# A seven-sweep graph kernel on one core: other order of the last two product phases, feature loads one phase ahead on another queue, separate count buffers, and a longer manual order at the start

## The chip, the cores and the metric

The kernel runs on one core of a Trainium2 chip. The metric is the device time of one execution in microseconds (us). The kernel before takes 3252.63 us (median of 3 runs, 3252.13 to 3258.63). The chips differ a little: in the rounds of the experiments the same kernel before took between 3253 and 3260 us (medians), so kernels of different rounds are compared by their ratio to the kernel before, not by their times.

## The reference

A graph network of four layers over one 2708 x 2708 adjacency `adj` and 2708 x 512 features `x`, all in float32. The heavy work is seven products of an adjacency-sized matrix with a feature-sized one. Cut to that:

```python
def _L0_gnn_ref(cur, incidence_m):
    head = (incidence_m > 0).astype(incidence_m.dtype)
    head = head / jnp.maximum(jnp.sqrt(jnp.sum(head * head, axis=-1, keepdims=True)), EPS)
    inc = incidence_m + head
    return (inc @ cur) / jnp.sum(inc, axis=-1, keepdims=True)          # sweep 0
# layer 1: adj @ x, and attn @ h with
#   e = where(adj != 0, exp(-leaky_relu(s_left[:, None] + s_right[None, :], 0.01)), 0)
# layer 2: p = adj_norm @ p, three times, each hop with its own weight
# layer 3: relu((dinv * (adj + I) * dinv @ x + x) @ W + b),  deg = max((adj != 0).sum(-1), 1)
x = _layernorm(x + _L0_gnn_ref(x, adj), axis=-1)                       # and so after each layer
```

In sweep 0 the row of `head` needs the number of positive entries of each row before the product can start, so every adjacency block is loaded once more to be counted. And the attention of layer 1 needs `s_left` as a column and `s_right` as a row; the kernel writes values made from the first as columns in sweep 0 and reads them back as rows later.

## The kernel before

Each of the seven products is a *sweep*. The 2708 nodes are split in halves, so the adjacency has four quarters 11, 12, 21, 22 and the features have four quarters B11, B12, B21, B22. A sweep goes over four ranges of adjacency columns; for each range seven products (P1 to P7) of the Strassen-Winograd kind replace eight. A product takes one *phase*, a range 7 phases, a sweep 28. The very first range is "plain": eight ordinary products. Positions in the listing are in phases from the start of a sweep. They set the order of the list; a scheduler may move an instruction ahead of its place.

```python
RANGES0 = [(768, 256), (0, 384), (384, 384), (1024, 330)]
PLAIN = dict(P1=0, P7=1, P5=2, P6=3, P4=4, P2=5, P3=6)
STAT = dict(P1="B11", P7="T3", P5="T1", P6="T2", P2="B21", P4="T4", P3="B22")
MOV = dict(P1="11", P7="s3", P5="21", P6="11", P2="12", P4="22", P3="11")
RING = 46
...
    def trans(nm):
        return pool.tile([P, 384], F32, name=nm, tag="ring", bufs=RING)
...
    # features of the next sweep: four quarters per tile, then the four sums T1 to T4
    def next_x(base, src, direct, sums=0.95, halves=0.50):
        for k in range(KT):
            late = (k * P) >= RANGES[-1][0]
            q = nc.gpsimd
            f = k / KT
            if not late:
                at(base - 5.8 + f, lambda k=k: x_load(src, k, "B11", q))
                at(base - 0.89 + f, lambda k=k: x_load(src, k, "B21", q))
                at(base - 0.88 + f, lambda k=k: x_load(src, k, "B22", q))
                at(base - 0.87 + f, lambda k=k: x_load(src, k, "B12", q))
                at(base - 0.6 + f, lambda k=k: x_sums(k))
...
    # counts of sweep 0: load, mask (ScalarE or VectorE), count by a product with ones
    def count_load(R0, n, h, i):
        w = wt(i % KT)
        t = trans("cl")
        j0 = (i // KT) * NH + (i % KT) * P
        nc.sync.dma_start(out=t[:w, :n], in_=adjT[j0 : j0 + w, h * NH + R0 : h * NH + R0 + n])
        cnt[R0, h, i] = t
```

When a tile of sweep 0 is done, two columns of 128 values are stored by GpSimd as rows of a matrix `SR` in memory:

```python
                for m in range(2):
                    nc.gpsimd.dma_start(out=SROW[R0, h][m : m + 1, lo : lo + w].rearrange("a i -> i a"),
                                        in_=rcol[:w, t, m : m + 1])
```

Adjacency tiles are loaded by SyncE into a ring of 46 buffers. At the end of the program, manual dependencies keep the instructions of the first range (`[:strict]`) in the order of the list on each engine.

## Time and profile before

| | before |
|---|---|
| time, median of 3 | 3252.63 us |
| profiled span | 3258.3 us |
| TensorE busy | 3152.8 us, 97% |
| VectorE, ScalarE, GpSimd busy | 1590.9, 564.8, 328.0 us |
| start to the first product | 47.6 us |
| four ranges of sweep 0 | 109.5, 126.1, 129.8, 114.0 us |
| first range of sweep 1 | 130.4 us (123.4 in the shortest run below) |
| last product of the last sweep to the end | 21.5 us |

The length of a range is read on TensorE's timeline, from its first product to the first product of the next range. With TensorE at 97%, only its waits and its slow spells can be won back; the prediction goes through them. Two views that the prediction does *not* use should have been read as well. The first is the list of DMA issues of the kernel before (columns: out<-in, engine, operation, number, KB each, median us from issue to landing):

```profile
SR<-rcol POOLq DMA_DIRECT2D x40, 0.5 KB, 9.1
```

A store of half a kilobyte takes 9.1 us, where a store of 256 KB (`X<-o`) takes a median of 3.5 us. There are 44 of these column stores (4 more of 0.3 KB). The second is the DMA view of the kernel before from 176 to 200 us, in 40 slices of 0.6 us (busy tenths of the DMA engines, then GB/s moved):

```profile
DMA  3957771099039675528999363895265364891167
GB/s 72 411 239 77 255 287 37 13 72 13 0 74 46 18 31 41 41 41 272 378 364 74 44 33 90 143 138 72 74 141 146 87 248 100 256 371 64 51 97 259
```

From the seventh to the eighteenth slice (179.6 to 186.8 us) some slices are 90% busy, and yet no more than 74 GB/s pass, where the 2nd, 3rd, 5th and 6th slices before them and the 19th to 21st after them show 239 to 411. Four column stores are issued between 177.8 and 181.7 us. In the trace's records of single packets, the data packets of SyncE's queue take a mean of 928 ns and up to 5346 ns from 180 to 182 us, against 82 ns in the 2 us before.

### The profile page before, as it was taken

What the parts mean: (1) busy time and instruction counts of PE and PEld (TensorE: products, weight loads), DVE (VectorE), ACT (ScalarE), POOL (GpSimd) and SP (SyncE); (2) the same over time, 40 slices, a digit from 0 to 9 for tenths busy, and PEclk for the clock granted to TensorE, in tenths of its full rate; (3) what the DMA queues carried; (4) which work ended last, traced back from release to release, by engine and by line L of the source; (5) the groups of instructions that cost most, each with busy time, mean ns of one, the idle gap of its engine ahead of it and who ended that gap; (6) DMA issues with size and microseconds to landing.
All of it is one profiled execution on the core that took longest, in us unless ns stands there. A gap on an engine that the chain in (4) does not pass through costs nothing. (4 is left out here: it accounts for less than half of the span.)

```text
span 3258.3 us, 35588 instructions
## 1 busy us (share of the span) xinstructions
PE 3152.8 (97%) x12090; PEld 2049.5 (63%) x12090; DVE 1590.9 (49%) x3914; ACT 564.8 (17%) x1096; POOL 328.0 (10%) x571
## 2 busy tenths in 40 slices
PE   4899998999999999999999999999999999899998
PEld 3656565556765555765556865568656587555675
DVE  5677596243356775865232333223254343543444
ACT  2543400000044544631000000000000000000000
POOL 0002013000000011113000020000111011300000
PEclk9999998999999999999999999999999999999999
DMA  5767566322343332544333453324434344533340
GB/s 168 190 176 140 152 136 108 87 64 53 94 88 113 114 114 90 152 138 148 102 87 87 122 153 101 104 65 124 137 115 139 98 135 131 171 116 95 106 128 30
DMA packets 268613, 380.42 MB, mean 117 GB/s; under 512 B 34824, under 2 KB 231008, under 8 KB 268432
## 3 DMA queue, kind: packets, MB, share of 16 engines
q1 hardware_dynamic: 232612, 293.00, 34.3%
q0 software_dynamic: 27104, 74.33, 7.2%
q10 hardware_dynamic: 8716, 10.84, 1.0%
q8 instruction: 95, 1.56, 0.2%
q14 instruction: 86, 0.70, 0.1%
HBM read 322.53 MB, written 55.49 MB: 116 GB/s over the span
## 5 line engine op out<-in xcount | busy, mean ns | idle before, releaser
L256 DVE TENSOR_TENSOR a<-a,a 128x384 f32<-128x384 f32 (+4 forms) x963 | 474.8, 509 | 333.3 <-PE accu L289 162.2
L289 PE MATMUL accu<-a,B 128*128 128x384 f32 (+5 forms) x1188 | 370.4, 457 | 0.0
L289 PE MATMUL acca<-a,B 128*128 128x384 f32 (+5 forms) x1188 | 362.2, 452 | 0.0
L289 PE MATMUL accc<-s,T 128*128 128x384 f32 (+5 forms) x1188 | 359.7, 455 | 0.0
L289 PE MATMUL accd<-a,B 128*128 128x384 f32 (+5 forms) x1188 | 356.2, 454 | 0.0
L289 PE MATMUL accd<-a,T 128*128 128x384 f32 (+5 forms) x1188 | 355.1, 457 | 0.0
L289 PE MATMUL accc<-a,T 128*128 128x384 f32 (+5 forms) x1188 | 352.5, 453 | 0.0
L289 PE MATMUL accu<-a,T 128*128 128x384 f32 (+5 forms) x1188 | 350.1, 452 | 0.0
L289 PEld LDWEIGHTS accd<-a,T 128*128 128x128 f32 (+1 forms) x1188 | 226.6, 192 | 113.6 <-issue 4.8
L289 PEld LDWEIGHTS accu<-a,T 128*128 128x128 f32 (+1 forms) x1188 | 223.4, 190 | 109.0
L289 PEld LDWEIGHTS accd<-a,B 128*128 128x128 f32 (+1 forms) x1188 | 222.4, 191 | 107.1 <-issue 4.0
L289 PEld LDWEIGHTS acca<-a,B 128*128 128x128 f32 (+1 forms) x1188 | 220.4, 190 | 109.7 <-issue 14.4
L289 PEld LDWEIGHTS accc<-a,T 128*128 128x128 f32 (+1 forms) x1188 | 222.3, 190 | 106.2
L289 PEld LDWEIGHTS accu<-a,B 128*128 128x128 f32 (+1 forms) x1188 | 219.8, 191 | 105.4 <-issue 14.4
L289 PEld LDWEIGHTS accc<-s,T 128*128 128x128 f32 (+1 forms) x1188 | 220.3, 190 | 103.4 <-issue 3.9
L256 DVE TENSOR_TENSOR s<-a,a 128x384 f32<-128x384 f32 (+4 forms) x321 | 162.0, 509 | 187.2 <-PE acca L289 121.2
L330 DVE TENSOR_TENSOR W<-W,accd 128x384 f32<-128x384 f32 (+2 forms) x54 | 27.3, 510 | 318.7 <-PE accd L289 317.2
L371 POOL TENSOR_TENSOR rstd<-rstd,neg_half 128x1 f32<-128x1 f32 (+1 forms) x88 | 52.0, 591 | 1031.9 <-DVE rstd L370 1026.2
L716 DVE TENSOR_TENSOR e<-e,f 128x384 f32<-128x384 f32 (+5 forms) x176 | 88.3, 506 | 81.4 <-ACT f L715 79.4
L330 DVE TENSOR_TENSOR C<-U,accc 128x384 f32<-128x384 f32 (+2 forms) x54 | 27.2, 509 | 204.1 <-PE accc L289 203.1
L323 ACT COPY U<-accu 128x384 f32<-128x384 f32 (+2 forms) x54 | 23.8, 443 | 572.7 <-PE accu L289 571.4
L714 ACT ACTIVATE e<-row,neg_s 128x384 f32<-128x384 f32 (+5 forms) x176 | 101.0, 574 | 101.6 <-DVE a L717 39.3
(199 smaller groups left out, 3104.5 us busy)
## 6 DMA issues: line engine op xcount, KB each, us to landing
a<-in_adjT SPq DMA_DIRECT2D x560, 192.0 KB
a<-in_adjT SPq DMA_DIRECT2D x280, 165.0 KB
a<-in_adjT SPq DMA_DIRECT2D x273, 128.0 KB
cl<-in_adjT SPq DMA_DIRECT2D x80, 192.0 KB
ld<-X SPq DMA_DIRECT2D x60, 256.0 KB
Y<-y POOLq DMA_DIRECT2D x54, 256.0 KB, 2.6
B<-Y POOLq DMA_DIRECT2D x84, 128.0 KB, 3.1
X<-o POOLq DMA_DIRECT2D x36, 256.0 KB, 3.5
```

Source lines behind the costliest of these rows:

```text
L256: nc.vector.tensor_tensor(A[r, dst, k][:w, :n], A[r, a, k][:w, :n], A[r, b, k][:w, :n], op)
L289: nc.tensor.matmul(B[home, c][:, :n], X[STAT[p], k][:w, c * P : (c + 1) * P], A[r, MOV[p], k][:w, :n], start=bool(start and k == k0), stop ...
L323: nc.scalar.copy(T[nm, c][:, :n], B[home, c][:, :n])
L330: nc.vector.tensor_tensor(d[:, :n], T[t, c][:, :n], o[:, :n], ALU.add)
L371: nc.gpsimd.tensor_tensor(rstd[:w, 1:2], rstd[:w, 0:1], neg_half[:w], ALU.pow)
L714: nc.scalar.activation(e[:w, :n], row[R0, h][0][:w, :n], AF.Exp, bias=neg_s[:w, t : t + 1])
L716: nc.vector.tensor_tensor(e[:w, :n], e[:w, :n], f[:w, :n], ALU.min)
```

## The change

Its intent: take the waits out of the start of the program, of the counts in sweep 0 and of the boundaries between sweeps. The diff cut to its core (cuts are marked):

```diff
-PLAIN = dict(P1=0, P7=1, P5=2, P6=3, P4=4, P2=5, P3=6)
+PLAIN = dict(P1=0, P7=1, P5=2, P6=3, P4=4, P3=5, P2=6)
-RING = 46
+RING = 43
...                               # x_sums: T4, the one that needs B21, goes to x_last
+    def x_last(k):
+        w = wt(k)
+        nc.vector.tensor_tensor(new_x("T4", k)[:w], X["B21", k][:w], X["T2", k][:w], ALU.subtract)
...
-    def next_x(base, src, direct, sums=0.95, halves=0.50):
+    def next_x(base, src, sums=0.95, halves=-0.25):
+        q = nc.sync
         for k in range(KT):
...
-            q = nc.gpsimd
...
                 at(base - 5.8 + f, lambda k=k: x_load(src, k, "B11", q))
-                at(base - 0.89 + f, lambda k=k: x_load(src, k, "B21", q))
-                at(base - 0.88 + f, lambda k=k: x_load(src, k, "B22", q))
-                at(base - 0.87 + f, lambda k=k: x_load(src, k, "B12", q))
-                at(base - 0.6 + f, lambda k=k: x_sums(k))
+                at(base - 1.85 + f, lambda k=k: x_load(src, k, "B22", q))
+                at(base - 1.84 + f, lambda k=k: x_load(src, k, "B12", q))
+                at(base - 1.55 + f, lambda k=k: x_sums(k))
+                at(base - 0.85 + f, lambda k=k: x_load(src, k, "B21", q))
+                at(base + 0.1 + f, lambda k=k: x_last(k))
             else:                 # tiles of the last range
-                at(base + halves + 0.05 * (k - 8), lambda k=k: x_load(src, k, "B21", q))
-                at(base + halves + 0.01 + 0.05 * (k - 8), lambda k=k: x_load(src, k, "B22", q))
+                at(base + halves + 0.05 * (k - 8), lambda k=k: x_load(src, k, "B22", q))
+                at(base + max(halves, 0.1) + 0.05 * (k - 8), lambda k=k: x_load(src, k, "B21", q))
...
-        t = trans("cl")
+        t = pool.tile([P, 384], F32, name="cl", tag="cl", bufs=3)
...
-        at(pb + (5.6 if r else 3.3), lambda: run_sums(R0, n, 0, inverse, r > 0))
+        at(pb + (5.2 if r else 3.3), lambda: run_sums(R0, n, 0, inverse, r > 0))
...                               # last sweep
-        order = (2, 3, 0, 1) if h else (0, 1, 2, 3)
+        order = (2, 3, 0, 1)
...
-    for i in list(nc.cur_bb.bb.instructions)[:strict]:
+    for n, i in enumerate(list(nc.cur_bb.bb.instructions)[:3 * strict]):
         if i.engine in last:
             tc.add_manual_dep(i, last[i.engine].name, ...)
-        last[i.engine] = i
+        if n < strict:
+            last[i.engine] = i
```

More of the change, by code (lines that the diff above doesn't have):

```diff
@@ L157, in x_sums @@
         b = b12.pop(k)
-        b11, b21, b22 = (X[s, k] for s in ("B11", "B21", "B22"))
-        for d, i, j in (("T1", b, b11), ("T2", b22, "T1"), ("T4", b21, "T2"), ("T3", b22, b)):
+        b11, b22 = X["B11", k], X["B22", k]
+        for d, i, j in (("T1", b, b11), ("T2", b22, "T1"), ("T3", b22, b)):
             j = X[j, k] if isinstance(j, str) else j
@@ L182, in x_load @@
         eng.dma_start(out=t[:w], in_=q)
-    def next_x(base, src, direct, sums=0.95, halves=0.50):
+    def next_x(base, src, sums=0.95, halves=-0.25):
+        q = nc.sync
         for k in range(KT):
-            late = (k * P) >= RANGES[-1][0]
-            q = nc.gpsimd
             f = k / KT
-            if not late:
+            if (k * P) < RANGES[-1][0]:
                 at(base - 5.8 + f, lambda k=k: x_load(src, k, "B11", q))
-                at(base - 0.89 + f, lambda k=k: x_load(src, k, "B21", q))
-                at(base - 0.88 + f, lambda k=k: x_load(src, k, "B22", q))
-                at(base - 0.87 + f, lambda k=k: x_load(src, k, "B12", q))
-                at(base - 0.6 + f, lambda k=k: x_sums(k))
-            else:
-                at(base + halves + 0.05 * (k - 8), lambda k=k: x_load(src, k, "B21", q))
-                at(base + halves + 0.01 + 0.05 * (k - 8), lambda k=k: x_load(src, k, "B22", q))
-                if not direct:
-                    at(base + 0.3 + 0.1 * (k - 8), lambda k=k: x_load(src, k, "B11", q))
-                    at(base + 0.31 + 0.1 * (k - 8), lambda k=k: x_load(src, k, "B12", q))
+                at(base - 1.85 + f, lambda k=k: x_load(src, k, "B22", q))
[3 more added lines that the diff above has]
+                at(base + 0.1 + f, lambda k=k: x_last(k))
+            else:
+                at(base + halves + 0.05 * (k - 8), lambda k=k: x_load(src, k, "B22", q))
+                at(base + max(halves, 0.1) + 0.05 * (k - 8), lambda k=k: x_load(src, k, "B21", q))
                 at(base + sums + 0.03 * (k - 8), lambda k=k: x_sums(k))
+                at(base + sums + 0.4 + 0.03 * (k - 8), lambda k=k: x_last(k))
     def next_ext(base, src):
@@ L216, in rest @@
                 x_sums(k)
+                x_last(k)
             at(base + 1.05 + 0.2 * (k - KT), rest)
@@ L614, in gnn_kernel @@
         at(6.0 + 0.9 * f, lambda k=k: x_sums(k))
+        at(7.5 + f, lambda k=k: x_last(k))
     at(2.6, start0)
     sweep(S[0], KT, RANGES0, prep=prep0, extra=extra0, done=done0, first=True, sums=True)
-    next_x(S[1], X1, True)
+    next_x(S[1], X1)
     W = {}
@@ L731, in extra2 @@
         at(pb - 1.0, lambda: rows(1))
-        at(pb + 5.6, lambda: run_sums(R0, n, 0, share))
+        at(pb + 5.2, lambda: run_sums(R0, n, 0, share))
         at(pb + 2.6, lambda: run_sums(R0, n, 1, share))
@@ L823, in gnn_kernel @@
     for s, hop, src, done in ((3, 2, Y0, hop_done(Y1)), (4, 1, Y1, hop_done(Y2)), (5, 0, Y2, done5)):
-        next_x(S[s], src, True, *((1.3, 0.95) if s == 3 else (0.95, 0.5)))
+        next_x(S[s], src, *((1.3, 0.3) if s == 3 else (0.95, -0.25)))
         next_ext(S[s], w_hop[hop])
         sweep(S[s], KT + 2, RANGES, done=done, ext_src=X2T, late=1.4 if s == 3 else 0.85)
-    next_x(S[6], X3, True)
+    next_x(S[6], X3)
     def start6():
@@ L853, in pre @@
             nc.vector.tensor_tensor(y[:, :n], y[:, :n], t[:, :n], ALU.add)
-        order = (2, 3, 0, 1) if h else (0, 1, 2, 3)
-        early = {(1, 2): -0.95, (1, 3): -0.9, (0, 0): -1.0, (0, 1): -0.95}
+        order = (2, 3, 0, 1)
+        early = {(1, 2): -0.95, (1, 3): -0.9, (0, 2): -1.05, (0, 3): -1.0}
         for j, c in enumerate(order):
```

## The prediction

> **What bounds the kernel now.** I began with the page, to see which engine is full:
>
> ```profile
> PE 3152.8 (97%) x12090; PEld 2049.5 (63%) x12090; DVE 1590.9 (49%) x3914; ACT 564.8 (17%) x1096; POOL 328.0 (10%) x571
> PE   4899998999999999999999999999999999899998
> PEclk9999998999999999999999999999999999999999
> ```
>
> TensorE has work in 97% of the span. The change removes no product: all seven products of each range stay, only the last two swap places. So it can only win back idle or slow TensorE time. Idle is 3258.3 - 3152.8 = 105.5 us, and the slices put it in the first fifth and in one slice near the end. The waits view of TensorE names it:
>
> ```profile
> PE acca L299 <- DVE a L498: 20.6, 1, 20.6
> PE cnt L460 <- DVE mask L447: 20.3, 21, 3.8
> PE cnt L460 <- ACT mask L450: 20.0, 8, 5.6
> PE deg L654 <- DVE mask L642: 15.6, 3, 12.3
> PE ps_n L400 <- DVE U L330: 10.9, 4, 9.6
> ```
>
> (Columns: total us, times, longest.) These five are 87.4 of the 105.5 us; the last products' epilogue is most of the rest. Each was then followed back on the timeline of the engine it names.
>
> Start (20.6 us), VectorE's timeline:
>
> ```profile
> 25.16 0.22 DVE L472 TENSOR_SCALAR r<-cnt 128x1 f32<-128x1 f32 x2 [0.31 <-PE cnt L460]
> 30.24 3.66 DVE L162 TENSOR_TENSOR T<-T,B 128x256 f32<-128x256 f32 x10 [4.86 <-DMA T<-in_x]
> ...
> 41.94 4.58 DVE L162 TENSOR_TENSOR T<-B,T 128x256 f32<-128x256 f32 x13 [6.55 <-DMA B<-in_x]
> 46.43 0.42 DVE L497 SCALAR_TENSOR_TENSOR s<-a,row 128x256 f32<-128x256 f32 x1
> ```
>
> L162 is the feature sums, listed for phase 6 but hoisted into the first range. VectorE runs in order, so the adjacency preparation (L497, L498) that the first product needs stands behind sums that wait for the last feature quarters. ScalarE had copied its `row` by 26.96 + 0.37 = 27.3 us; the preparation starts at 46.4 and the first product at 47.58.
>
> Counts (20.0 us): ScalarE's timeline shows the masks waiting for the count tiles' load, here the longest:
>
> ```profile
> 328.32 0.48 ACT L449 ACTIVATE mask<-cl 128x330 bf16<-128x330 f32 x1 [7.17 <-DMA cl<-in_adjT]
> ```
>
> SyncE's timeline has 13 `cl` issues spread over 18.3 us from 313.6, against about 0.33 us for an issue that does not wait: the count tiles queue for slots of the ring that the adjacency tiles fill.
>
> First sweep boundary (15.6 us), TensorE, then VectorE:
>
> ```profile
> 522.61 0.24 PE L654 MATMUL deg<-ones_bf,mask 128*128 128x1 bf16 x3 [12.26 <-DVE mask L642]
> 510.30 0.43 DVE L162 TENSOR_TENSOR T<-B,T 128x256 f32<-128x256 f32 x1 [7.19 <-DMA B<-X]
> 517.30 0.43 DVE L162 TENSOR_TENSOR T<-B,T 128x256 f32<-128x256 f32 x1 [5.91 <-DMA B<-X]
> ```
>
> The next sweep's feature quarters load in the last phase, because the last product holds B22; GpSimd's issues alternate between waiting for TensorE, for VectorE and behind its small normalisation powers. VectorE, in order, stops at the sums and the masks behind them are late. The last boundary is the same (`ps_n` at 2818.42, 9.61 us, after `B<-X` waits in the chain). The four boundaries between lose about 1 us each or nothing.
>
> Two windows tell what else is near its limit:
>
> ```profile
> 160.00:200.00 40.00, 34.54 (x140) 20.59 (x138) 36.50 (x94) 13.89 (x28) 4.91 (x8) 0.94 0.79 170
> 520.00:560.00 40.00, 33.83 (x175) 21.14 (x176) 29.30 (x103) 2.76 (x6) 15.54 (x26) 0.84 0.42 64
> ```
>
> (Busy us of PE, PEld, DVE, ACT, POOL; granted clock; DMA share; GB/s.) At 160 to 200 us VectorE is busy 36.5 of 40. In both, the clock fell below 1.
>
> **What the Trainium skill says.** "TensorE: Matmul & The Clock Gate", section "What's actually happening": after an idle window of about 3.4 us the array runs at half clock until a busy one has passed. The trace agrees: after the 5.60 us wait at 329 us, twelve products of 128x384 take 6.89 us against 3.87 us elsewhere. So each long stall costs about 3 us more, and I count it with the stall. "DMA: Bandwidth & Descriptors", section "Issuing engines are not separate DMA queues": all issuers share the same 16 engines, and another issuer saves only issue time. So going from GpSimd to SyncE buys no bandwidth; it frees GpSimd (0.54 us busy per load in its timeline, a median 4.3 us from issue to landing for `B<-X`). "Advanced Engine Details and Errata", section "Sequencer Loop": a sequencer reads instructions one after the other. The trace agrees in the hoisted sums above; on SyncE it is also a risk.
>
> **The change part by part.**
>
> 1. *First range kept in order.* The manual dependencies now also hold the instructions listed up to three times as far behind the last one of the first range, which covers the sums at phase 6. Preparation can start at 27.3 instead of 46.4 us: 0.8 us for the first tile, first product at about 28.6. That is 47.6 - 28.6 = 19.0 us. Feeding it: B21 is issued from 19.8 to 26.1 us and needed one phase later (44 products of 0.216 us = 9.5 us); B22 had landed by about 42 to 46 us and is needed after three phases, about 59. So data should not stop it. But 33 subtractions (11 tiles of T1, T2, T4) at about 0.35 us, 11.6 us, return to VectorE between phases 6 and 8.5, just where it is 91% busy. I charge 4 us. Net 15.
>
> 2. *Count tiles in three buffers of their own, ring 46 to 43.* Waits at 188.9, 195.5, 318.7 and 329.4: 0.47 + 4.35 + 1.26 + 5.60 = 11.7 us, plus two half-clock spells of about 3.4 = 18.5 us. Count loads no longer hold ring slots, but stand in the same SyncE queue as adjacency loads that do, and three buffers allow no burst; near 195 us VectorE would set the pace anyway. I take 10. The waits in the first range (92.9 to 111.7 us, about 10 us idle) come from weight loads issued on ScalarE and from sums of weights; those stay.
>
> 3. *Order P3, P2, with B22 and B12 loaded and T1, T2, T3 formed one phase earlier; B21 and T4 later.* The last phase now holds only B21, which feeds T4, needed at phase 4. First boundary: 12.26 + 2.52 + 0.80 us of waits, and the window's clock of 0.84 gives 0.16 x 40 = 6.4 us, together 22. I take 18; masks and late tiles of the last range stay. Last boundary: 9.61 us and about 2.8 of slow clock; I take 11.
>
> 4. *Cost of the swap.* P3 needs 11-12, formed after the load of "12". Setting the third group of L256 against the start of the sixth phase, those combinations end before it in all 27 ranges (245.2 against 246.9 us in the tightest), so P3 one phase earlier should not wait. Moving the row sums from 5.6 to 5.2 is small for the same reason. The final epilogue mirrors the old one: 0.
>
> 5. *Smaller ring and the shared queue*: -1 to -5 us, most likely in the third sweep, where exponent tiles use the ring too. Freed GpSimd: +1 to 2. Together -2.
>
> Sum: 15 + 10 + 18 + 11 - 2 = 52; 3252.6 - 52 = 3200.6. The author has placed each event in fractions of a phase, which looks tuned on the chip, so I lean 2 us further: 3199.
>
> **Rivals.** *VectorE becomes the bound of the first sweep.* For: 36.5 of 40 us, and the sums come back there. Against: from 100 to 160 us the same windows show it busy 44.6 of 60. Then 1 and 2 give 10 instead of 25 us: about 3214. *SyncE's queue blocks at its head*: a feature load that waits for TensorE holds the next adjacency loads behind it. For: its timeline already has 32 `a` loads spread over 86.7 us from 498.9. Against: "11" slots are free a phase earlier in the new order, and no adjacency load is listed between the "12" loads and the last phase. Boundary gains would halve, and waits appear in the middle boundaries: about 3220. *All stalls vanish*: 19 + 18 + 22 + 12 = 71, with some of the first range's 10 us: about 3178, faster by over 2%. *Transfers hidden anyway*: the middle boundaries, a third of what was rewritten, gain nothing; already in the sum.
>
> **Range and chances.** The four gains are nearly independent, each uncertain by 4 to 7 us, together about 12, and I widen that for the rivals: 3178 to 3222. Two per cent is 65 us, 3187.6; that needs nearly every stall gone: 0.30. Within: 0.67. Slower: 0.03, as it would need new stalls of over 100 us.
>
> **What would show it.** Right: first acca product near 28 to 30 us; no mask wait for `cl` over 3 us after 160; PE waits of `deg` and `ps_n` at the two boundaries below 4 us; granted clock 0.95 or more in the window of the first boundary; `B<-X` gone from GpSimd. Wrong: waits of L289 for DVE L256 or L498 in the first sweep, waits for L162 sums at boundaries, new waits for `a` loads in the third sweep, or clock dips at other places.

## The result

The changed kernel takes 3272.39 us (median of 4 runs, 3267.95 to 3274.05) against 3253.01 us of the kernel before in the same rounds (4 runs, 3252.13 to 3258.63). The ratio is 1.0054 with a 95% interval of 1.0036 to 1.0071. Ratios in this document are the mean time of one kernel's runs over the mean of the other's in the same rounds, so they are not quite the ratio of the medians. The prediction of 3199 us is missed by 73 us, and the range by 50: instead of a gain of 54 us there is a loss of some 18.

The page of the changed kernel, whose profiled span is 3272.1 us (busy us of each engine; then, in 40 slices, the busy tenths of TensorE and the clock granted to it, in tenths of full speed):

```profile
PE 3172.4 (97%) x12090; PEld 2059.3 (63%) x12090; DVE 1593.8 (49%) x3914; ACT 571.2 (17%) x1096; POOL 225.4 (7%) x381
...
PE   6899998999999999999999999999999999899998
...
PEclk9899998999999999999999999999999999999999
```

The first slice went from 4 to 6 tenths, so the start is indeed shorter. GpSimd went from 328.0 to 225.4 us and from 571 to 381 instructions: the feature loads have left it. TensorE is busy 19.6 us *longer* with the same 12090 instructions, which is time at a slower clock: the clock record has 101.7 us at half speed, against 66.2 before, and half of the difference is 17.7 us. Its waits in the changed kernel (total us, times, longest; `cnt` is a count, `deg` a degree count, `ps_n` and `ps_t` are transposes of finished tiles, `accd` one of the large products, `ps_d` a product with a weight matrix):

```profile
PE cnt L463 <- ACT mask L453: 23.1, 9, 6.8
PE cnt L463 <- DVE mask L450: 19.5, 21, 4.0
PE ps_n L403 <- DVE P1c L333: 11.2, 2, 9.4
PE ps_t L409 <- DVE o L381: 10.4, 3, 9.1
PE accd L292 <- DVE a L259: 5.3, 3, 3.9
PE deg L658 <- DVE mask L646: 5.1, 2, 4.3
...
PE ps_d L417 <- DVE P1c L857: 2.7, 1, 2.7
```

Of the five lines of the prediction, the 20.6 us before the first product are gone. The other waits have moved rather than vanished: `deg` fell from 15.6 to 5.1 us, but `ps_t` (10.4), `accd` (5.3) and `ps_d` (2.7) are new, the waits of the counts for ScalarE's masks grew from 20.0 to 23.1 us, and the wait of `ps_n` at the last boundary is still there, at 9.4 instead of 9.6 us. The window of the first boundary (same columns as in the prediction) has not recovered either:

```profile
520.00:560.00 40.00, 32.91 (x176) 21.05 (x176) 25.16 (x89) 1.58 (x3) 9.09 (x15) 0.81 0.53 125
```

The granted clock there is 0.81, where it was 0.84.

The ledger of the two profiled runs, from the first products on TensorE's timeline, in us:

| stretch | before | after | difference |
|---|---|---|---|
| start to the first product | 47.6 | 27.6 | -20.0 |
| first range (plain) | 109.5 | 126.9 | +17.4 |
| second range | 126.1 | 125.8 | -0.3 |
| third range | 129.8 | 132.2 | +2.4 |
| last range of sweep 0 | 114.0 | 128.5 | +14.5 |
| first range of sweep 1 | 130.4 | 125.5 | -4.9 |
| from there to the last sweep | 2148.5 | 2149.7 | +1.2 |
| first range of the last sweep | 124.5 | 123.9 | -0.6 |
| rest of its ranges | 306.4 | 306.5 | +0.1 |
| epilogue | 21.5 | 25.5 | +4.0 |
| span | 3258.3 | 3272.1 | +13.8 |

So the start won what was predicted and the first range gave nearly all of it back; the last range of sweep 0 lost more than its boundary won; the epilogue lost 4 us. The traces name what stands behind each.

**First range.** ScalarE's waits in the kernel before, for the load of a count tile, over the whole run:

```profile
ACT mask L449 <- DMA cl<-in_adjT: 27.4, 7, 7.2
```

The same line after:

```profile
ACT mask L452 <- DMA cl<-in_adjT: 59.1, 28, 7.6
```

Seven waits have become 28, and 13 of these, 23.8 us, are in the first range. SyncE's own waits in the first range of the changed kernel (60 to 155 us) say why:

```profile
SPq L442 <- ACT mask L452: 46.5, 41, 10.6
```

The issue of a count load now waits for the mask that frees one of three buffers, 41 times.

**Last range of sweep 0.** SyncE's timeline after (start, us, engine, line, operation, out<-in, number):

```profile
433.56 2.28 SPq L249 DMA_DIRECT2D a<-in_adjT  x5
446.38 0.33 SPq L186 DMA_DIRECT2D B<-X  x1
446.81 14.43 SPq L249 DMA_DIRECT2D a<-in_adjT  x9
```

Between 435.84 (the end of the first line) and 446.38 SyncE issues nothing. It stands at one feature load; the program's order says that it is the B11 quarter of tile 5. Nine adjacency loads are behind it. GpSimd's timeline shows what the load waits for, the store of that same tile, and what the store waits among:

```profile
434.82 1.12 POOL L581 DMA_DIRECT2D SR<-rcol  x2 [0.56 <-DVE rcol L579]
435.93 0.54 POOL L393 DMA_DIRECT2D X<-o  x1
438.17 1.07 POOL L581 DMA_DIRECT2D SR<-rcol  x2 [1.70 <-DVE rcol L579]
```

The store `X<-o` sits between two pairs of column stores, and by the trace it lands at 446.36 us, 10.4 us after its issue. VectorE then runs out of adjacency tiles, at a load that SyncE issued right after it had stood (446.81) and that took 9.4 us more to land:

```profile
456.26 0.50 DVE L500 SCALAR_TENSOR_TENSOR s<-a,row 128x330 f32<-128x330 f32 x1 [8.58 <-DMA a<-in_adjT]
```

**First boundary.** At the end of that range the same happens again: SyncE stands 13.3 us, from 505.07 to 518.40, at a feature load that waits for an `X<-o` store. VectorE's timeline waits first for a fetch of `in_x` and then for the late B21:

```profile
517.86 0.75 DVE L557 SCALAR_TENSOR_TENSOR ld<-ps_n,rd,ld 74x512 f32<-74x512 f32 x1 [9.16 <-DMA ld<-in_x]
...
536.20 0.43 DVE L167 TENSOR_TENSOR T<-B,T 128x256 f32<-128x256 f32 x1 [7.82 <-DMA B<-X]
```

TensorE pays for the first of these with the 9.1 us of `ps_t` in its waits. The standing queue did not make this fetch late: SyncE had issued it at 503.63, before it stood, and it landed only at 517.84. The B21 load was as slow (issued 525.01, landed 536.18). These two waits are slow transfers, with column stores in flight, and not late issues.

**Last boundary.** SyncE, VectorE and TensorE in turn, each from its own timeline:

```profile
2805.42 7.24 SPq L186 DMA_DIRECT2D B<-X  x3
```

```profile
2814.02 0.43 DVE L167 TENSOR_TENSOR T<-B,T 128x256 f32<-128x256 f32 x1 [5.63 <-DMA B<-X]
```

```profile
2828.32 0.88 PE L403 MATMUL ps_n<-ident,P1c 128*128 128x128 f32 x2 [9.41 <-DVE P1c L333]
```

Three feature loads take 7.24 us to issue (0.33 us each when they do not wait), VectorE stands in order at T4, and the additions that feed the last tiles are behind it. Within the 7.24 us SyncE stands 5.9 us at a load that waits for an `X<-o` store. The first load that VectorE waits for was issued before that (2804.67) and took 9.3 us to land, so the block is not the whole of this wait.

**Epilogue.** TensorE after, at the output product of the last tiles:

```profile
3249.21 3.55 PE L417 MATMUL ps_d<-w,P1c 128*128 128x512 f32 x4 [2.66 <-DVE P1c L857]
```

Four products take 3.55 us where others of the form take 1.88, after a wait of 2.66.

### The profile page after: what moved, and what is told of

It reads as the page before. It is cut to its first block, busy times and chain, and to the rows that moved or that the text cites. A ratio compares the mean times of both kernels' runs of the same rounds, so it can differ in the third digit from the quotient of the medians.

```text
span 3272.1 us, 35367 instructions
## 1 busy us (share of the span) xinstructions
PE 3172.4 (97%) x12090; PEld 2059.3 (63%) x12090; DVE 1593.8 (49%) x3914; ACT 571.2 (17%) x1096; POOL 225.4 (7%) x381
## 4 chain that ended last, share of the span: by engine, by line
PE 88%; DMA 5%; DVE 3%; issue 1%; ACT 1%; POOL 0%; SPq 0%; ACTq 0%; POOLq 0%; DVEq 0%
PE accu L292 22%; PE accc L292 21%; PE accd L292 21%; PE acca L292 10%; PE ps_d L417 9%; DMA cl<-in_adjT 2%; PE ps_n L403 1%; DMA a<-in_adjT 1%; PE ps_t L409 1%; PE acca L302 1%; DMA ld<-in_x 1%; PE pz L683 1%; ACT mask L452 1%; DMA B<-in_x 0%; DMA B<-X 0%
## 5 line engine op out<-in xcount | busy, mean ns | idle before, releaser
L259 DVE TENSOR_TENSOR a<-a,a 128x384 f32<-128x384 f32 (+4 forms) x963 | 475.8, 510 | 370.0 <-DMA a<-in_adjT 194.9
L292 PEld LDWEIGHTS accu<-a,B 128*128 128x128 f32 (+1 forms) x1188 | 220.8, 192 | 107.4 <-issue 16.8
L259 DVE TENSOR_TENSOR s<-a,a 128x384 f32<-128x384 f32 (+4 forms) x321 | 161.9, 509 | 209.9 <-PE accd L292 102.6
L333 DVE TENSOR_TENSOR W<-W,accd 128x384 f32<-128x384 f32 (+2 forms) x54 | 27.1, 509 | 276.1 <-PE accd L292 262.3
L333 DVE TENSOR_TENSOR C<-U,accc 128x384 f32<-128x384 f32 (+2 forms) x54 | 27.1, 509 | 195.1 <-PE accc L292 193.7
```

Source lines behind the costliest of these rows:

```text
L259: nc.vector.tensor_tensor(A[r, dst, k][:w, :n], A[r, a, k][:w, :n], A[r, b, k][:w, :n], op)
L292: nc.tensor.matmul(B[home, c][:, :n], X[STAT[p], k][:w, c * P : (c + 1) * P], A[r, MOV[p], k][:w, :n], start=bool(start and k == k0), stop ...
L333: nc.vector.tensor_tensor(d[:, :n], T[t, c][:, :n], o[:, :n], ALU.add)
```

## The experiments

Four theories came out of this, against the prediction's own reasons as rivals.

- **A.** The column stores of sweep 0, which both kernels have, slow every other transfer for some 6 us each time. The waits that the prediction put down to ring slots (count tiles) and to the place of the feature loads (first boundary) were waits for these transfers. Rival: ring slots and places, as predicted.
- **B.** Three count buffers end the run-ahead of the count loads that the ring allowed. Rival: the subtractions that came back to VectorE made the first range long.
- **C.** SyncE issues in order; a feature load that waits for a store of `X` holds the adjacency loads and fetches behind it. Rivals: the new product order, or the earlier loads by themselves.
- **D.** The new order of the last sweep finishes feature chunks 0 and 1 last, but the output product still takes them first. Rival: the epilogue is longer for another reason.

All kernels gave correct results. The expectations sometimes count the ranges of a sweep from 0; the text and the tables count them from 1. In the names, "b" is the kernel before with something added, "a" the changed kernel with something altered. Times and ratios, with the median of the kernel before in the same rounds:

| run | median us | before | ratio to before, 95% |
|---|---|---|---|
| changed kernel | 3272.39 | 3253.01 | 1.0054 [1.0036, 1.0071] |
| b_twice | 3307.89 | 3254.25 | 1.0165 [1.0149, 1.0181] |
| b_rows | 3228.85 | 3260.24 | 0.9902 [0.9887, 0.9917] |
| a_rows | 3220.92 | 3260.24 | 0.9878 [0.9863, 0.9893] |
| b_strict | 3236.88 | 3254.25 | 0.9946 [0.9932, 0.9961] |
| a_clring | 3255.02 | 3260.24 | 0.9986 [0.9971, 1.0000] |
| a_pool | 3276.48 | 3260.24 | 1.0045 [1.0028, 1.0061] |
| a_clring_late | 3255.71 | 3259.63 | 0.9990 [0.9973, 1.0007] |
| a_clring_pool | 3250.12 | 3259.63 | 0.9966 [0.9951, 0.9981] |
| a_b11 | 3273.55 | 3259.74 | 1.0039 [1.0023, 1.0056] |
| a_clring_b11 | 3248.69 | 3259.74 | 0.9965 [0.9950, 0.9980] |
| a_rows_lateq | 3212.34 | 3254.25 | 0.9870 [0.9853, 0.9886] |
| a_dense (one look, state unknown) | 3280.87 | 3259.74 | none |
| a_clring_rows | 3207.86 | 3259.63 | 0.9837 [0.9822, 0.9852] |
| b_strict_rows | 3209.44 | 3259.63 | 0.9841 [0.9827, 0.9856] |
| best1 | 3197.78 | 3254.25 | 0.9827 [0.9812, 0.9842] |

The stretches in their profiled runs, in us, as in the ledger:

| run | first product | range 1 | range 2 | range 3 | last of sweep 0 | first of sweep 1 | epilogue |
|---|---|---|---|---|---|---|---|
| before | 47.6 | 109.5 | 126.1 | 129.8 | 114.0 | 130.4 | 21.5 |
| changed | 27.6 | 126.9 | 125.8 | 132.2 | 128.5 | 125.5 | 25.5 |
| b_twice | 45.0 | 125.8 | 130.9 | 140.2 | 133.4 | 132.4 | 21.5 |
| b_rows | 46.1 | 109.5 | 118.3 | 120.3 | 102.2 | 125.4 | 21.5 |
| a_rows | 27.9 | 115.3 | 118.5 | 120.2 | 105.1 | 123.4 | 25.7 |
| b_strict | 26.8 | 109.4 | 127.0 | 128.9 | 114.1 | 130.0 | 21.4 |
| a_clring | 27.0 | 109.3 | 128.9 | 135.6 | 124.5 | 125.1 | 24.0 |
| a_pool | 28.4 | 126.0 | 127.6 | 140.4 | 125.0 | 130.5 | 25.2 |
| a_clring_late | 27.5 | 110.7 | 127.2 | 132.7 | 126.0 | 125.2 | 24.0 |
| a_clring_pool | 26.4 | 111.2 | 129.8 | 126.6 | 119.9 | 131.3 | 25.4 |
| a_b11 | 28.1 | 128.4 | 128.7 | 136.3 | 124.3 | 126.4 | 25.7 |
| a_clring_b11 | 29.2 | 110.9 | 129.9 | 133.3 | 116.9 | 126.4 | 25.7 |
| a_rows_lateq | 26.9 | 117.5 | 118.6 | 120.2 | 105.4 | 123.4 | 25.6 |
| a_dense | 27.5 | 128.4 | 128.3 | 139.6 | 125.7 | 128.3 | 21.6 |
| a_clring_rows | 27.1 | 109.2 | 118.4 | 120.6 | 101.7 | 125.2 | 27.4 |
| b_strict_rows | 28.4 | 109.5 | 118.5 | 120.2 | 105.0 | 126.0 | 21.5 |
| best1 | 26.8 | 110.0 | 118.5 | 120.5 | 101.0 | 123.4 | 21.4 |

A control for reading it: the changed kernel and a_dense differ only in the last epilogue, yet their third ranges are 132.2 and 139.6 us, in different rounds (and a_dense is the look of unknown state). While the column stores are there, a single range of one profile says little below some 7 us. Without them, ranges 2 and 3 repeat within 0.4 us over six kernels.

### Theory A: the column stores

**b_twice**: the kernel before, each column store issued twice.

```diff
-                for m in range(2):
+                for m in (0, 1, 0, 1):
                     nc.gpsimd.dma_start(out=SROW[R0, h][m : m + 1, lo : lo + w].rearrange("a i -> i a"),
```

> The kernel before, with each column store of the first sweep issued twice (88 instead of 44, the same values; nothing else moves). Theory A: the waits grow with the number of column stores; taking them away saved some 31 us, so doubling them costs 15 to 40 us, ratio 1.005 to 1.012, all of it before 660 us. If their shape is harmless and it was only TensorE's and ScalarE's new place that helped in the row variant: within 4 us of before.

Measured: 3307.89 us, ratio 1.0165. That is 0.0165 x 3254 = 54 us for 44 more stores, 1.2 us per store, though they move 22 KB in all. It is in the expected direction and larger than the 15 to 40 us expected. All four ranges of sweep 0 grew, by 16.3, 4.8, 10.4 and 19.4 us; the first product and the epilogue did not.

**b_rows** and **a_rows**: TensorE transposes the two columns of a tile into two rows, ScalarE copies them, and one store writes two contiguous rows of 512 bytes.

```diff
-                for m in range(2):
-                    nc.gpsimd.dma_start(out=SROW[R0, h][m : m + 1, lo : lo + w].rearrange("a i -> i a"),
-                                        in_=rcol[:w, t, m : m + 1])
...                               # ps: the bank of tile "pg", made wider and handed on
+            def e(t=t, lo=lo, w=w, got=got):
+                ps = got["pg"]
+                nc.tensor.transpose(ps[:2, P : P + w], rcol[:w, t, :], ident[:w, :w])
+                s = small.tile([2, P], F32, name="srow", bufs=3)
+                nc.scalar.copy(s[:, :w], ps[:2, P : P + w])
+                nc.gpsimd.dma_start(out=SROW[R0, h][:, lo : lo + w], in_=s[:, :w])
...
+            at(p + 0.9, e)
```

For the kernel before:

> The kernel before, with the same row stores in place of the column stores. Theory A: the waits after 157 us for count tiles (11.7 us and two half-clock spells) and the first sweep boundary (22 us with its slow clock) go, the time falls from 3253 to about 3220. If the ring and the late feature loads were the cause, as my prediction had it, it stays within 5 us of 3253.

For the changed kernel:

> The changed kernel, with the 44 column stores of the first sweep (SR, 128 elements of 4 bytes each[...]) written instead as 22 row stores: TensorE turns the two columns, ScalarE copies them, one store of two rows. Theory A (the column stores hold up all other DMA traffic for some 6 us each, and that is what the count masks and the first sweep boundary wait for): the first range shrinks from 127.1 us to about 112, the last range of the first sweep from 128.5 to about 115, waits of the masks for count tiles fall from 59 us to under 25, and the time falls from 3272 to about 3230. Theory B (three count buffers) and theory C (feature loads that block SyncE's queue): the masks still wait, and the time stays within 8 us of 3272.

Measured: b_rows 0.9902, so 32 us faster than before; a_rows 0.9878, which against the changed kernel's 1.0054 is 1.76% or 57 us. The DMA issues of a_rows:

```profile
SR<-srow POOLq DMA_DIRECT2D x20, 1.0 KB, 2.9
```

The same values land in 2.9 us instead of 9. In b_rows, with ring, places and queues of the kernel before untouched, ranges 2 and 3 fall by 7.8 and 9.5 us, and the last range with its boundary by 11.8 + 5.0. So A holds in both directions, more stores and none, and the rival falls: no ring slot and no load was moved in b_rows. The packet records agree. Between the first product and the end of sweep 0, 399 packets of SyncE's queue take more than 1 us in the kernel before, 559 in b_twice and 14 in b_rows (of some 45000 in each). As these are SyncE's own loads, the time that GpSimd spends on issuing its stores does not explain them. The stores cost the changed kernel about 57 - 32 = 25 us more than the kernel before.

### Theory B: three count buffers

**b_strict**: the kernel before with the longer manual order alone.

```diff
-    for i in list(nc.cur_bb.bb.instructions)[:strict]:
+    for n, i in enumerate(list(nc.cur_bb.bb.instructions)[: 3 * strict]):
...
-        last[i.engine] = i
+        if n < strict:
+            last[i.engine] = i
```

> The kernel before, with the longer manual order alone (the change's part 1). The first product starts near 28 us instead of 47.6. Theory B (it was the three count buffers that gave this gain back): the first range keeps its 109.6 us and the whole is about 19 us faster than before, ratio 0.994. Rival (the order itself gives it back, as the sums return to VectorE): the first range or the second grows by 10 us or more and the ratio is 0.998 or above.

Measured: ratio 0.9946, 17.6 us. The first product comes at 26.8 us and range 1 stays at 109.4. So the subtractions that come back to VectorE cost nothing there, which removes the rival of B.

**a_clring**: the changed kernel with the count tiles in the ring again.

```diff
-RING = 43
+RING = 46
-        t = pool.tile([P, 384], F32, name="cl", tag="cl", bufs=3)
+        t = trans("cl")
```

> The changed kernel with the count tiles back in the ring of 46. Theory B (three buffers take away the run-ahead that covered slow stretches of DMA): the first range shrinks from 127.1 us to about 112 as the kernel before has it (109.6), and the time is about 3257. If the buffers are not it: 127 us and 3272.

Measured: ratio 0.9986; range 1 falls from 126.9 to 109.3 us, as in the kernel before. TensorE's waits in range 1 (60 to 155 us) of the changed kernel:

```profile
PE cnt L463 <- ACT mask L453: 16.5, 5, 6.8
```

And in range 1 (60 to 137 us) of a_clring:

```profile
PE cnt L463 <- ACT mask L453: 7.5, 3, 2.9
```

B is shown, with one limit: the edit gives the ring its three buffers back at the same time, and the ring of 43 was not tried alone. Even without column stores three buffers cost something: range 1 takes 115.3 us in a_rows and 109.2 in a_clring_rows.

### Theory C: the head of SyncE's queue

What a_clring leaves is a last range of 124.5 us against 114.1 in b_strict.

**a_pool**: the changed kernel, all feature loads of `next_x` on GpSimd as before, at their new places.

```diff
-        q = nc.sync
+        q = nc.gpsimd
```

> The changed kernel with the feature loads of the six sweeps back on GpSimd's queue, at their new places. Theory C (a feature load that waits for a stored feature blocks the adjacency loads behind it on SyncE): the last range of the first sweep shrinks from 128.5 us to about 116, the waits at 435 and 458 us go, and the time is about 3260. Theory A alone: the range stays at 125 or more and the time within 4 us of 3272.

Measured: ratio 1.0045, not distinguishable from the changed kernel. VectorE's wait for adjacency tiles in the last range falls from 8.6 to 3.8 us, but the last range, at 125.0 us, is no shorter than in the control (125.7). Moving everything back does not help as it stands, so this run missed its expectation and does not support C as a whole.

**a_clring_late**: a_clring with B22, B12 and the first sums back at their old places, still on SyncE.

```diff
-                at(base - 1.85 + f, lambda k=k: x_load(src, k, "B22", q))
-                at(base - 1.84 + f, lambda k=k: x_load(src, k, "B12", q))
-                at(base - 1.55 + f, lambda k=k: x_sums(k))
+                at(base - 0.88 + f, lambda k=k: x_load(src, k, "B22", q))
+                at(base - 0.87 + f, lambda k=k: x_load(src, k, "B12", q))
+                at(base - 0.6 + f, lambda k=k: x_sums(k))
```

> The changed kernel with the count tiles back in the ring of 46, and the loads of B22 and B12 and the first three sums moved back one phase (to 0.88 and 0.87 phases before the next sweep, sums at 0.6), still on SyncE's queue; the new product order stays. Theory C (a feature load placed a phase earlier stands in SyncE's queue before the adjacency loads and holds them while it waits for the store of X, itself slowed by the column stores): the wait of VectorE for adjacency tiles in the last range of sweep 0 (9.8 us in the run with the ring alone) falls below 3, and that range from 124.5 to 114 to 117 us; the first boundary is then again as long as before, range 0 of sweep 1 about 130 instead of 125. Time 3248 to 3253, against 3255. Rival (the new order of the products itself makes the last range longer): it stays at 123 to 126 us, time 3253 to 3260.

Measured: 3255.71 us, last range 126.0. This was a miss. VectorE's waits in the last range:

```profile
DVE s L500 <- DMA a<-in_adjT: 11.9, 3, 10.3
```

The same wait as in a_clring (11.1, longest 9.8). The order of SyncE's queue explains the miss: it stands 10.2 us there, as in a_clring (10.4), and the load at its head is a B11 quarter, whose place neither the diff nor this run moved. The expectation had named the wrong quarter. The run does show that the earlier *places* of B22 and B12 are not what makes the range long.

**a_clring_pool**: a_clring with all feature loads on GpSimd (the edit of a_pool).

> The changed kernel with the count tiles back in the ring of 46, and all feature loads of the next sweeps back on GpSimd's queue, in their new earlier places. Theory C: SyncE no longer stands at a feature load, so VectorE's wait for adjacency tiles in the last range falls below 4 us and that range to 115 to 120; but on GpSimd the loads now stand before the row stores and column stores, so ranges 1 and 2 may lengthen by some us (with three count buffers range 2 went from 132 to 140). Time 3248 to 3258. Rival (the earlier place loses the time on any queue, since the loads share the engines with the adjacency loads): last range 123 to 126 us, time 3255 to 3262.

Measured: 3250.12 us, ratio 0.9966. The wait for adjacency tiles is gone from the last range, which falls from 124.5 to 119.9 us. A new one takes its place in VectorE's waits there:

```profile
DVE o L381 <- POOL rstd L374: 11.0, 3, 10.0
```

GpSimd now stands at the feature loads, and its small powers for the layer norm behind them are late. The head of a queue blocks on GpSimd as it does on SyncE; only what stands behind is different.

**a_b11** and **a_clring_b11**: only the B11 loads back on GpSimd, in the changed kernel and in a_clring.

```diff
-                at(base - 5.8 + f, lambda k=k: x_load(src, k, "B11", q))
+                at(base - 5.8 + f, lambda k=k: x_load(src, k, "B11", nc.gpsimd))
```

> The changed kernel with only the B11 loads of the next sweeps back on GpSimd's queue; B22, B12, B21 stay on SyncE, all in their new places. Theory C, made sharper by the run that moved B22 and B12 back without effect: what stood 10.5 us at the head of SyncE's queue at 436 us is the B11 load of feature tile 5, waiting for the store of that tile; the diff did not move its place, only its queue. Then VectorE's wait for adjacency tiles in the last range of sweep 0 falls from 8.6 us to under 3, that range from 128.5 us to 115 to 120, time 3260 to 3266 against 3272. Rival (the early B22 and B12 loads, or the new order, make the last range long): that range stays at 126 us or more, time 3269 to 3276.

> The same with the count tiles back in the ring of 46. Theory C: last range of sweep 0 from 124.5 us to 113 to 117, time 3243 to 3248 against 3255, and no 10 us wait of VectorE for GpSimd's rstd as in the run with all feature loads on GpSimd. Rival: last range 122 to 126, time 3252 to 3258.

Measured: a_clring_b11 3248.69 us with a last range of 116.9 us, and neither the wait for adjacency tiles nor the one for `rstd` (2.7 us at most) in it. The range is within what C expected, the time 0.7 us above. a_b11 missed: 3273.55 us, last range 124.3 (125.7 in the control). There SyncE stands 15.7 us, until 432.0, at another feature load (a B12 quarter) that also waits for an `X<-o` store. This does not explain the miss: in a_clring_b11 SyncE stands 18.8 us at such a load, until the same point of the range (10 us after its start), and no wait for adjacency tiles follows. Why the last range of a_b11 stays long is open. So C is shown for the ring version only. The intervals of a_clring and a_clring_b11 overlap, so for C the proof lies in the named waits that come and go with the edit, more than in the times.

### The last boundary

**a_rows_lateq**: a_rows with the B22 and B21 loads of the last range's tiles on GpSimd.

```diff
-                at(base + halves + 0.05 * (k - 8), lambda k=k: x_load(src, k, "B22", q))
-                at(base + max(halves, 0.1) + 0.05 * (k - 8), lambda k=k: x_load(src, k, "B21", q))
+                at(base + halves + 0.05 * (k - 8), lambda k=k: x_load(src, k, "B22", nc.gpsimd))
+                at(base + max(halves, 0.1) + 0.05 * (k - 8), lambda k=k: x_load(src, k, "B21", nc.gpsimd))
```

> The changed kernel with row stores, and with the late feature loads alone (B22 and B21 of the last three tiles, which wait for features just stored) back on GpSimd's queue. Theory C for the last boundary (these six loads wait for stores at the head of SyncE's queue, B21 of the other tiles stands behind them, and with it VectorE's last difference and the sum that the transposes need): the wait of ps_n for P1c, 10.0 us, falls under 3, with its half clock 10 to 12 us, ratio about 0.985 against 0.988 of the row variant. If the stores themselves are late: the wait stays at 8 us or more.

Measured: ratio 0.9870 against 0.9878 of a_rows; the times alone cannot tell them apart. TensorE's waits at the last boundary (2740 to 2890 us) of a_rows:

```profile
PE ps_n L403 <- DVE P1c L333: 10.0, 1, 10.0
```

And of a_rows_lateq:

```profile
PE ps_t L409 <- DVE o L381: 3.5, 1, 3.5
```

The long wait is gone, as expected, and a shorter one comes in elsewhere. The last range of sweep 5 and the first of sweep 6 together take 225.4 us instead of 231.0 (before 229.8, changed 230.9). So the six late loads on SyncE's queue made the long wait at the last boundary. The edit wins 5.6 us where 10 to 12 were expected, and against the kernel before it wins 4.4 of the 11 us that were predicted.

### Theory D: the epilogue

**a_dense**: the changed kernel, the output product of the last sweep in the order in which its chunks become ready.

```diff
-    def dense(lhs, wts, w):
+    def dense(lhs, wts, w, order=(0, 1, 2, 3)):
         ps = bank("ps_d")
-        for c in range(DC):
-            nc.tensor.matmul(ps[:w], lhs(c), wts[c], start=c == 0, stop=c == DC - 1)
+        for c in order:
+            nc.tensor.matmul(ps[:w], lhs(c), wts[c], start=c == order[0], stop=c == order[-1])
...                               # last sweep: dense(..., W[6], w, (2, 3, 0, 1))
```

> The changed kernel with the output product of the last sweep summing its four feature chunks in the order 2, 3, 0, 1. Theory D (the new order finishes chunks 0 and 1 last, and the output product still takes them first): the waits of the output product for chunk 0 or 1 in the epilogue, 2.7 us, go below 1, and from the end of the last sweep product to the end is 21 to 22 us instead of 25.5. Rival: it stays near 25. The time itself moves by 4 us at most, less than one look can tell.

Measured: the epilogue is 21.6 us instead of 25.5, and TensorE goes through without a wait:

```profile
3257.26 3.60 PE L417 MATMUL ps_d<-w,U 128*128 128x512 f32 x8
```

Eight products in 3.60 us, where the changed kernel's first four took 3.55. D is shown; best1 below repeats the length (21.4 us).

### What the rest of the change is worth

**a_clring_rows**: the changed kernel with row stores and the ring of 46. **b_strict_rows**: the kernel before with row stores and the longer manual order. They differ by the product order, the feature loads, the row sums and the epilogue.

> The changed kernel with row stores and with the count tiles back in the ring of 46: the change as it is without its own count buffers and without the column stores that hold the other transfers up. From the run with row stores (3221): first range 115.4 to 109.6, so about 3214 to 3216, ratio 0.985 to 0.986. Compared with the kernel before plus the longer manual order plus row stores it tells what the new order and the earlier feature loads are worth by themselves: if those were worth what the prediction says (18 + 11 us at two boundaries), this is 25 us or more faster than that one; by theories A and C, which say that the boundaries were the column stores' doing, it is within 8 us of it, and 4 us of the epilogue are lost.

> The kernel before with row stores and with the longer manual order only. Run with row stores alone: 0.9902; the longer manual order alone: 0.9946. If both gains are independent, 0.985 (3204 to 3208), first product at 27 us, first range 109 to 110. If the feature loads of the old places still cost the boundaries what the prediction says, the changed kernel with row stores and ring is 25 us or more faster; else about equal or slower.

Measured in the same rounds: 3207.86 and 3209.44 us, ratios 0.9837 and 0.9841, not distinguishable. In the profiles, from the end of the first range to the last product of the last sweep, the first takes 3042.5 us and the second 3049.0, 6.5 us in favour of the change; the epilogue takes 5.9 of these back. So the part for which the prediction had 18 + 11 us is worth about 6.5 us once the column stores are gone. The last range of sweep 0 also shows how C depends on A. With column stores it is 124.5 us in a_clring against 114.1 in b_strict; without them it is 101.7 us in a_clring_rows against 105.0 in b_strict_rows, with the feature loads still in SyncE's queue. The queue's head costs something in sweep 0 only while the stores that it waits for land late.

### A version that beats both

**best1**: the changed kernel with row stores (a_rows), the ring of 46 (a_clring), the late tiles on GpSimd (a_rows_lateq) and the matching order of the output product (a_dense).

> The changed kernel with row stores, count tiles in the ring of 46, late loads on GpSimd, and the last dense products in the order in which their inputs get ready (2, 3, 0, 1). Expected from the single runs: first product at 28 us, first range 110 us instead of 115 (theory B), last boundary 10 us shorter (theory C), epilogue after the last product of the sweeps 21.5 instead of 25.5 us (theory D, a mirror that did not mirror). Together some 20 us below the row variant, ratio about 0.981.

Measured: 3197.78 us, ratio 0.9827 [0.9812, 0.9842]. The last boundary gave 5.4 us (231.0 to 225.6) where 10 were expected. The kernel is 1.7% faster than the kernel before and 2.3% faster than the changed one (0.9827 / 1.0054 = 0.977). TensorE is busy 3140.9 of 3194.5 us.

## Why the prediction was wrong

**Part 1, the first range in order: right.** Predicted 19.0 us for the start, less 4 for VectorE. The start won 20.0, and b_strict shows 17.6 us in all with range 1 unchanged at 109.4 us. The charge of 4 us was not needed.

**Part 2, count tiles: the failed step with the wrong sign.** "The count tiles queue for slots of the ring" was read from 13 issues spread over 18.3 us. The waits for count tiles after 160 us were real, and their size, 18.5 us with the slow spells, was right: b_rows wins 7.8 + 9.5 = 17.3 us in those ranges. But it wins them with the ring untouched. What was late was the transfer, not its issue: the tile that the mask at 328.32 waits for, in the line that the prediction shows, was the first of those 13 loads, issued at 313.62, and it landed at 328.30, when four column stores also landed (328.1 to 328.9). The ring had allowed the count loads to run ahead; "three buffers allow no burst" is in the text, and was charged as a smaller gain when it was a loss of 17.4 us.

**Part 3, the boundaries: the failed step with the wrong cause.** The size was right again at the first: 18 us predicted, and b_rows wins 11.8 + 5.0 = 16.8 there. But it wins them with all feature loads in their old places. The loads landed late with the column stores in flight: the two that the prediction's lines wait for were issued at 501.30 and 502.77 and landed at 510.28 and 517.28, after 9.0 and 14.5 us, where the median is 4.3. Issuing them elsewhere did not change that. The change won 4.9 us in the first range of sweep 1 and lost 14.5 in the range before it. At the last boundary, 11 us were predicted and -1.1 came (229.8 to 230.9 us for two ranges): there the late loads now stood in SyncE's queue (a_rows_lateq).

**Part 4, the swap costs nothing: right but for the epilogue.** "The final epilogue mirrors the old one: 0" overlooked that the output product did not turn with it: +4.0 us.

**Part 5, ring and shared queue: mis-sized.** -2 us were charged, spread over the third sweep. That sweep is unharmed (the whole stretch from sweep 1 on is +1.2 us), but the last range of sweep 0 is 124.5 us in a_clring against 114.1 in b_strict, and taking B11 off SyncE's queue alone brings it to 116.9. The shared queue cost some 8 us there, and only with the column stores.

**The rivals.** "SyncE's queue blocks at its head" is what happened, in sweep 0 and at the last boundary. It was set aside because no adjacency load is *listed* between the "12" loads and the last phase. The argument looked at the loads that were moved and not at B11, whose place stayed but whose queue changed, and at waits for TensorE, when the load waits for a store. Its estimate of 3220 halved the boundary gains; it never let them turn negative. "VectorE becomes the bound" fell with b_strict.

**The skill's statements.** "TensorE: Matmul & The Clock Gate", "What's actually happening", agrees on the slow speed after a wait, but not on its length: the page names an idle window of about 3.4 us, and here four products that take 1.88 us elsewhere took 3.55 us after a wait of 2.66. "DMA: Bandwidth & Descriptors", "Issuing engines are not separate DMA queues", says that the transfers of all issuers run on the same 16 engines and interleave. That fits what the runs show, GpSimd's column stores slowing SyncE's loads, and the prediction used it only to say that a change of issuer brings no bandwidth. The same page, "Rules for kernel authors", says that a strided last dimension becomes one descriptor per element and should be made contiguous. The trace agrees with the advice (0.5 KB in 9.1 us, against 1 KB in 2.9 us as rows). The descriptors themselves it does not show: a column store appears as 16 packets of 32 bytes, a row as one of 512. Had this row been held against the list of DMA issues, the cause could have been seen before.

**What the prediction's own signs said.** Of its five, first product near 28 and feature loads gone from GpSimd came true. No mask wait over 3 us after 160 (7.63 at 327.5), boundary waits below 4 us (`deg` 4.3 and `ps_n` 9.4, with a new `ps_t` of 9.1) and a clock of 0.95 (0.81) did not. Of its signs of failure two appeared under the new line numbers: "waits for L162 sums at boundaries", on L167, and a product waiting for the combinations of L256 in the first sweep (`accd` for L259, 5.3 us).

**What stays open.** Why a column store slows the packets of other queues is not shown, only that it does. The row stores change three things at once, the size of a run, the number of stores and the path through TensorE, so which of size and number counts was not separated. That a_pool was no faster than the changed kernel is only partly explained, by GpSimd's own queue, and that a_b11 was not is unexplained.

## What to carry to other kernels

When a load lands late, look first at what else is in the DMA engines at that moment, above all at stores of few bytes with a long time to landing, before moving the load or giving it more buffers: here the change moved loads, their queue and their slots against a disturbance that a transpose and a contiguous store removed. A load that waits for a store may share a queue only with work that can afford to wait as long as it. And separate buffers for a stream are a limit as well as a protection: count how far the stream ran ahead in the shared ring before giving it three of its own.

## What the Trainium skill lacked or had wrong

- "DMA: Bandwidth & Descriptors", section "Rules for kernel authors", advises against a strided last dimension, but neither this nor the section "Why small descriptors are slow (HBM only)" says that *other* transfers suffer. The passage on turns between queues ("Queues, rings and completion order") has no figure or warning for it either. Here 44 stores of up to 128 four-byte elements cost the kernel before 32 us and the changed one 57 us, and doubling them cost 54 us; packets of another queue took up to 5.3 us during them.
- The same page, section "Issuing engines are not separate DMA queues", says that several issuers only save the time to initiate a DMA. It does not say what choosing an issuer can cost, and the timelines of "Perfetto Trace Analysis" do not draw what a waiting DMA means for the loads behind it. Here SyncE stood 10.5 and 13.3 us at such loads, and GpSimd delayed VectorE by 10.0 us when they were moved there.
- "TensorE: Matmul & The Clock Gate", section "What's actually happening", gives one idle window of about 3.4 us as what brings half speed. In the changed kernel waits of 2.66 us (epilogue), 2.79 us (at 74.9) and 3.05 us (at 122.7) were followed by a granted clock of 0.5 as well. (The ends of products are modelled in the trace, so these waits are not exact.)
- No page has a rule for the depth of a stream's own buffers against a shared ring. Three instead of up to 46 cost 17.4 us in one range with column stores, and 115.3 - 109.2 = 6.1 us without.
